# Splitting the last store of a pairwise product kernel into groups of 16 partitions

## Chip, cores, metric

One core of one Trainium2 chip. Times are device microseconds of a whole execution; lower is better. A verdict is "faster" or "slower" beyond 2%. The profile's span is some 1.8 us shorter than the timed execution of the same run.

## The reference

```python
# x: (4096, 32, 64) float32, W: (64, 64) float32
vid = jnp.einsum('bfd,de->bfe', x, W)
idx_i, idx_j = jnp.triu_indices(32, k=1)          # 496 pairs of fields
return x[:, idx_i, :] * vid[:, idx_j, :]          # (4096, 496, 64), 520 MB
```

Almost all the traffic is the result: 520 MB written, 34 MB read.

## The kernel before

A tile holds 256 rows of the batch: 128 partitions are 2 halves x 64 elements, and each pair of fields has 128 values (512 B) per partition. TensorE forms `vid` in PSUM, VectorE multiplies, and SP stores the products, 124 pairs at a time (63,488 B in each of 128 partitions) once the kernel is under way. Three output buffers are in rotation.

```python
    for t in range(NT):                       # 16 tiles of 496 pairs
        ...                                   # loads on the ACT queue, matmuls
        sent = 0
        for j in range(1, F):
            i = 0
            while i < j:
                ...                           # ot: [128, 124, 128], one of 3 buffers
                nc.vector.tensor_tensor(ot[...], xt[...], vid[...], ALU.mult)
                i += n
                at += n
                if t * NP + at == until or at in (base + SLOT, NP):
                    nc.sync.dma_start(
                        out=out[t][:, sent:at, :],
                        in_=ot[:, sent - base : at - base, :],
                    )
                    sent = at
```

## Time and profile before

| | before |
|---|---|
| time, median of the first 3 runs (least, most) | 1298.64 us (1297.97, 1299.37) |
| span of the profiled run | 1296.3 us |
| VectorE's waits for stores to free a buffer | 149.5 us in 52 waits |
| one row of 63,488 B on one DMA engine | 2.342 us, 27.1 B/ns |

The last row is from the trace's records of DMA packets. These, and the records of semaphore updates, give each transfer's shares of work (each of the 82 stores has 128 rows and 16 updates; a "share" is what stands behind one update, and is read as what one engine does of one transfer), though without the engines' numbers. The lines of the profile, and what they say of the end of the program, are in the prediction.

### The profile page before, as it was taken

What the parts mean: (1) busy time and instruction counts of PE and PEld (TensorE: products, weight loads), DVE (VectorE), ACT (ScalarE), POOL (GpSimd) and SP (SyncE); (2) the same over time, 40 slices, a digit from 0 to 9 for tenths busy, and PEclk for the clock granted to TensorE, in tenths of its full rate; (3) what the DMA queues carried; (4) which work ended last, traced back from release to release, by engine and by line L of the source; (5) the groups of instructions that cost most, each with busy time, mean ns of one, the idle gap of its engine ahead of it and who ended that gap; (6) DMA issues with size and microseconds to landing.
All of it is one profiled execution on the core that took longest, in us unless ns stands there. A gap on an engine that the chain in (4) does not pass through costs nothing.

```text
span 1296.3 us, 2062 instructions
## 1 busy us (share of the span) xinstructions
PE 225.5 (17%) x512; PEld 52.1 (4%) x512; DVE 1098.1 (85%) x544; POOL 0.2 (0%) x4
## 2 busy tenths in 40 slices
PE   4112131122121121211212112121121211212000
PEld 1000000000000000000000000000000000000000
DVE  7999999898798888988888888888888888979970
POOL 0000000000000000000000000000000000000000
PEclk8555555565555555655555565555555655555555
DMA  9999999999999999999999999999999999999996
GB/s 379 430 426 433 438 432 425 434 434 434 428 432 432 434 432 434 431 434 436 432 434 434 426 434 432 430 432 432 432 433 431 434 432 434 432 431 443 425 431 288
DMA packets 20891, 553.81 MB, mean 427 GB/s; under 512 B 2448, under 2 KB 2448, under 8 KB 10256
## 3 DMA queue, kind: packets, MB, share of 16 engines
q1 hardware_dynamic: 12816, 524.33, 93.8%
q10 hardware_dynamic: 8064, 29.36, 5.5%
q8 instruction: 4, 0.07, 0.0%
q14 instruction: 7, 0.06, 0.0%
HBM read 33.59 MB, written 520.09 MB: 427 GB/s over the span
## 4 chain that ended last, share of the span: by engine, by line
DMA 61%; DVE 34%; issue 1%; DVEq 0%; PE 0%; SPq 0%
DMA out_dram<-o 61%; DVE o L99 34%; DMA x<-in_r_x_dram 0%; DVEq L145 0%; PE pv L81 0%; DVEq L99 0%; SPq L56 0%
## 5 line engine op out<-in xcount | busy, mean ns | idle before, releaser
L99 DVE TENSOR_TENSOR o<-x,pv 128x2176 f32<-128x2176 f32 (+27 forms) x544 | 1098.1, 2093 | 158.3 <-DMA out_dram<-o 149.5
L81 PE MATMUL pv<-x,w 64*64 64x512 f32 x512 | 225.5, 1025 | 966.3 <-DMA x<-in_r_x_dram 887.2
L81 PEld LDWEIGHTS pv<-x,w 64*64 64x64 f32 x512 | 52.1, 208 | 1138.0 <-issue 1137.4
L128 POOL MEMSET const-bfloat16-1.0<- 128x1 bf16 x1 | 0.1, 102 | 0.0
L128 POOL MEMSET const-uint8-127<- 128x1 uint8 x1 | 0.1, 102 | 0.0
L128 POOL MEMSET const-float32-1.0<- 128x1 f32 x1 | 0.1, 99 | 0.0
L128 POOL MEMSET const-float32-0.0<- 128x1 f32 x1 | 0.1, 98 | 0.2 <-issue 0.2
## 6 DMA issues: line engine op xcount, KB each, us to landing
out_dram<-o SPq DMA_DIRECT2D x56, 7936.0 KB, 42.9
x<-in_r_x_dram ACTq DMA_DIRECT2D x56, 512.0 KB, 48.7
out_dram<-o SPq DMA_DIRECT2D x2, 3008.0 KB, 17.8
out_dram<-o SPq DMA_DIRECT2D x1, 5952.0 KB, 27.1
out_dram<-o SPq DMA_DIRECT2D x1, 4928.0 KB, 23.1
out_dram<-o SPq DMA_DIRECT2D x1, 4416.0 KB, 19.0
out_dram<-o SPq DMA_DIRECT2D x1, 4224.0 KB, 21.2
out_dram<-o SPq DMA_DIRECT2D x1, 3904.0 KB, 15.3
```

The lines of the kernel that those rows point to most:

```text
L81: nc.tensor.matmul(pv[half, :, :], lhsT=w2[half, :], rhs=xt[half, b : b + BANK, :], start=True, stop=True,)
L99: nc.vector.tensor_tensor(ot[:, at - base : at - base + n, :], xt[:, i : i + n, :], vid[j // BANK][:, j % BANK : j % BANK + 1, :].to_broad ...
L128: nc = _bacc.Bacc("TRN2", target_bir_lowering=False, num_devices=1, dynamic_dma_scratch_size=1024)
```

## The change

The change stores the last 124 pairs in eight groups of 16 partitions, each without its last 1 to 8 pairs, and deals those out in stores of 15 and 1, 14 and 2, ... 8 and 8 partitions. A small store leaves some engines out, and the change takes work from some and gives it to others, evidently so that they all end together. Where the texts say "high-numbered", take it as those that the small stores leave out.

```diff
+def steps(lo, hi):
+    for g in range(8):
+        yield lo, hi - g - 1, 16 * g, 16 * g + 16
+    for g in range(8):
+        yield hi - g - 1, hi, 16 * g, 16 * g + 15 - g
+        yield hi - g - 1, hi, 16 * g + 15 - g, 16 * g + 16
...
-                    nc.sync.dma_start(
-                        out=out[t][:, sent:at, :],
-                        in_=ot[:, sent - base : at - base, :],
-                    )
+                    last = t == NT - 1 and at == NP
+                    for lo, hi, p, q in steps(sent, at) if last else [(sent, at, 0, P)]:
+                        nc.sync.dma_start(
+                            out=out[t][p:q, lo:hi, :],
+                            in_=ot[p:q, lo - base : hi - base, :],
+                        )
```

## The prediction

> **What bounds the kernel now.** I read the page first, for the span, the strip of 40 slices and the bytes:
>
> ```profile
> span 1296.3 us, 2062 instructions
> PE 225.5 (17%) x512; PEld 52.1 (4%) x512; DVE 1098.1 (85%) x544; POOL 0.2 (0%) x4
> DMA  9999999999999999999999999999999999999996
> GB/s 379 430 426 433 438 432 425 434 434 434 428 432 432 434 432 434 431 434 436 432 434 434 426 434 432 430 432 432 432 433 431 434 432 434 432 431 443 425 431 288
> HBM read 33.59 MB, written 520.09 MB: 427 GB/s over the span
> ```
>
> The reader is to see that the DMA engines are 90% busy or more in every slice but the last, which falls to 6 tenths and 288 GB/s. VectorE, at 85%, waits for buffers that stores free. The kernel is bound by the DMA engines, and what the change touches is the end of the last slices. So next come the waits of the SP queue (who waited for whom: us in total, times, longest) and the timeline at the end:
>
> ```profile
> SPq L145 <- DMA out_dram<-o: 38.5, 1, 38.5
> ```
>
> ```profile
> 1239.46 16.95 DVE L99 TENSOR_TENSOR o<-x,pv 128x768 f32<-128x768 f32 x5 [1.69 <-DMA out_dram<-o]
> ```
>
> VectorE ends its last product at 1239.46 + 16.95 = 1256.41 us; after that SP does nothing but wait for the last store to land. How the 16 engines run out is in the busy table by windows (columns: window, length, PE, PEld, DVE, POOL, clock, DMA share, GB/s):
>
> ```profile
> 1260.00:1265.00 5.00, 0.00 (x0) 0.00 (x0) 0.00 (x0) 0.00 (x0) 0.50 1.00 432
> 1275.00:1280.00 5.00, 0.00 (x0) 0.00 (x0) 0.00 (x0) 0.00 (x0) 0.50 0.94 406
> ...
> 1284.00:1286.00 2.00, 0.00 (x0) 0.00 (x0) 0.00 (x0) 0.00 (x0) 0.50 0.37 159
> 1286.00:1288.00 2.00, 0.00 (x0) 0.00 (x0) 0.00 (x0) 0.00 (x0) 0.50 0.07 32
> 1288.00:1290.00 2.00, 0.00 (x0) 0.00 (x0) 0.00 (x0) 0.00 (x0) 0.50 0.22 95
> 1290.00:1291.00 1.00, 0.00 (x0) 0.00 (x0) 0.00 (x0) 0.00 (x0) 0.50 0.15 63
> ```
>
> (A window counts a packet where it starts, so shares jump.) From 1284 us on few engines still have work. The semaphore updates in the trace give it engine by engine: the 16 shares of the last store land from 1283.29 to 1295.48 us, eight of them by 1284.1, the last two at 1294.85 and 1295.48; their mean is about 1286.7. The store before it landed with the same pattern, from 1264.58 to 1276.76. So the engines are out of step by 12.2 us, the same in each of the last six stores, and the end is set by one slow engine that still has its eight rows to do. In the packet records each row of 63,488 B takes 2.342 us on one engine (27.1 B/ns), on slow engines too: they are late, not slower here. Perfect balance would be worth 1295.5 - 1286.7 = 8.8 us, 0.7%, and that is the ceiling of any gain at this end.
>
> The cost of an issue, from the view of the tensor that the stores write:
>
> ```profile
> L108 SPq DMA_DIRECT2D out_dram<-o x82: 332/332/348, 12.2 to 1256.4; - x82
> ```
>
> The three durations (least, median, most) are in ns: 332 for nearly all. The next SP instruction starts 0.38 us after an issue.
>
> [...] All 82 stores before have 128 partitions and land in 16 shares[...]. [...] The trace doesn't number its engines; it only shows that all 16 run at 27.1 B/ns together. [...]the first packet of the 32 KB weight load starts 1.0 us after its issue, and the last data packet's end to its landing is 0.35 us, so a small store should take some 1.45 us.
>
> **The change part by part.** One store of 128 rows x 124 pairs becomes 24: eight of 16 partitions with 123 down to 116 pairs, then for each group the last 1 to 8 pairs in two parts (15 and 1, 14 and 2, ... 8 and 8 partitions). Bytes, VectorE, TensorE and everything before 1256.4 us stay as they are; the compared orders of the two built programs show only SP gaining 22 rows.
>
> *Moved bytes.* With one partition to an engine, each engine gets eight leading rows of 956 pairs together instead of 992. [...] A pair is 512 B, 19 ns at 27.1 B/ns, so the most that a late engine is relieved of is 36 x 19 = 0.68 us. That is the gain, if the late engines are the high-numbered ones: the slowest would land its leading rows at about 1294.85.
>
> *New waits.* In the built program each store waits for the one that used its semaphore before, and there are eight: store 8 waits for the former last but one store (landed 1276.76), store 9 for store 1, and so on to store 24 for store 16. Before, such waits were few; they show as stores that wait for a load whose semaphore they reuse, though they need nothing of it:
>
> ```profile
> SPq L108 <- DVE o L99: 1168.4, 80, 22.2
> SPq L108 <- DMA x<-in_r_x_dram: 50.3, 5, 19.1
> ```
>
> Now store 8 is issued at about 1276.8 and its rows can start at 1277.8; the fast engines run out of the first seven at 1264.24 + 7 x 2.27 = 1280.1, so that is just hidden. But store 16 can go only when store 8 has landed on the slowest engine, 1294.9, and stores 17 to 24 follow at 0.385 us each: the last is issued at 1294.9 + 8 x 0.385 = 1298.0 and lands 1.45 us later, at 1299.5. Against 1295.5 that is +4.0 us: without anything else, 1298.6 + 4 = 1302.7 us.
>
> [...] Then the time is 1325 to 1338, about 1332 us.
>
> **Rivals.** (A) [...]my main theory, chance 0.68: 1325 to 1340. [...]against: no transfer of this trace has fewer than 128 partitions[...]. (B) An engine's rate is the only limit and the chain of semaphores sets the end, chance 0.27: 1302.7. For it: the waits are in the built program; the ports' effect is unseen here. (C) [...]1309 to 1318; chance 0.04. (D) The relief of the high engines is all that counts, and SP's issues are hidden: 1298; chance 0.01, since store 24 cannot be issued before store 16 has landed.
>
> **Range and chances.** 2% is 26 us, so slower begins at 1324.6. A gives slower nearly always, with a small part of it just below the line; B and C give the same; a gain over 2% would need three times the whole imbalance. I put the prediction at 1331 us, a little below the middle of A as B pulls the median down; the range 1300 to 1342 holds B's and A's values. Faster 0.01, same 0.33, slower 0.66.
>
> **What would show it.** For A: packets of some 62,000 B in the last 60 us that take 4 to 9 us in place of 2.34, a DMA share still high but GB/s near 110 to 200, the end of the span at about 1330. For B: packets at 2.3 us, the leading rows landing by 1295, SP waiting at the store line for earlier stores, a last issue at about 1298. In both, SP's waits for stores at the store line must appear. I am wrong if the last issue comes without waiting, if SP's issues of small stores cost far from 0.385 us, or if the slow engines' lag differs in the changed run.

The sum came to this: 1298.6 us for the kernel before; with 4.0 us for the chain of semaphores 1302.7 us; and, by the main theory, with 26 to 39 us (34 in the middle, the chain included) in place of the 4.0, 1325 to 1338, about 1332 us. The main theory (A), the ports theory, supposed that the engines slow one another when a store has few partitions.

## The result, and the profile after

The changed kernel takes 1320.47 us (median of 4 runs, 1317.48 to 1324.50) against 1298.76 us (4 runs), +21.7 us. The ratio is 1.017, with a 95% interval of 1.0141 to 1.0198: "same" by the 2% rule, but a clear loss. A ratio here is the mean time of one kernel's runs over that of the other's of the same rounds, so not quite the ratio of the medians.

The profiled run is the slowest of the four (1324.5 us). Its page shows where the time goes: the strip of 40 slices is as before until the last two, which move 269 and 109 GB/s where before they moved 431 and 288.

```profile
span 1322.7 us, 2085 instructions
DMA  9999999999999999999999999999999999999994
GB/s 379 427 426 433 439 436 427 427 448 427 427 429 450 424 427 428 449 427 426 425 445 430 425 432 444 426 428 432 440 425 427 437 439 425 429 445 430 432 269 109
```

The busy table by windows at the end, first of the kernel before, then of the changed kernel (columns as in the prediction, the last three are clock, DMA share and GB/s):

```profile
1264.00:1282.00 18.00, 0.00 (x0) 0.00 (x0) 0.00 (x0) 0.00 (x0) 0.50 1.03 444
```

```profile
1264.40:1282.00 17.60, 0.00 (x0) 0.00 (x0) 0.00 (x0) 0.00 (x0) 0.50 1.08 200
1282.00:1300.00 18.00, 0.00 (x0) 0.00 (x0) 0.00 (x0) 0.00 (x0) 0.50 0.89 237
1300.00:1318.00 18.00, 0.00 (x0) 0.00 (x0) 0.00 (x0) 0.00 (x0) 0.50 0.23 67
1318.00:1322.00 4.00, 0.00 (x0) 0.00 (x0) 0.00 (x0) 0.00 (x0) 0.50 0.28 55
```

This is the reading that matters most. From 1264.4 to 1282 us the engines are as busy as before (1.08 against 1.03), and they move less than half as much (200 against 444 GB/s). The first line starts 0.4 us earlier; from 1264.4 us on, the kernel before has 1.01 and 436 GB/s. A busy engine is not a fast one here: rows take longer. In the packet records, 84 of the 183 rows after 1258 us still run at 27 B/ns (37 of them before the first group's rows start); the others are slower and take up to 15.5 us in place of 2.3.

The waits of the SP queue show the second part of the loss:

```profile
SPq L119 <- DVE o L108: 1169.8, 80, 22.2
SPq L119 <- DMA x<-in_r_x_dram: 49.3, 5, 19.0
SPq L119 <- DMA out_dram<-o: 42.5, 8, 20.8
SPq L156 <- DMA out_dram<-o: 1.3, 4, 0.4
```

The third line is new: eight times SP waits at the store line (L119) for an earlier store, 42.5 us in all, where before it waited 38.5 us at the end of the program. These are the waits for a semaphore that is used again. The last of them ends when store 8 has landed on the last engine at 1317.45; store 16 is issued at 1317.47, store 24 at 1320.13, and it has landed at 1321.88.

### The profile page after: what moved, and what is told of

Its sections match the earlier page's. It is cut to its first block, busy times and chain, and to the rows that moved or that the text cites. A ratio compares the mean times of both kernels' runs of the same rounds, so it can differ in the third digit from the quotient of the medians.

```text
span 1322.7 us, 2085 instructions
## 1 busy us (share of the span) xinstructions
PE 225.8 (17%) x512; PEld 52.1 (4%) x512; DVE 1098.0 (83%) x544; POOL 0.2 (0%) x4
## 4 chain that ended last, share of the span: by engine, by line
DMA 60%; DVE 33%; issue 1%; DVEq 0%; PE 0%; SPq 0%
DMA out_dram<-o 60%; DVE o L108 33%; DMA x<-in_r_x_dram 0%; DVEq L156 0%; PE pv L90 0%; DVEq L108 0%; SPq L65 0%
```

## The experiments

Each replaces only `steps` (for e4 also the slice of partitions). All results were correct, and all timed runs of the fast state (e6 and e7 have one run each, of unknown state). Two questions: do the few partitions of each store make the loss (the ports theory), or the chain of semaphores; and why is the loss smaller than the estimate?

**e1: the groups alone, no split tails.**

```diff
-    for g in range(8):
-        yield lo, hi - g - 1, 16 * g, 16 * g + 16
-    ... (the tails)
+    for g in range(8):
+        yield lo, hi, 16 * g, 16 * g + 16
```

> The eight groups of 16 partitions with all 124 pairs each, and no split tails: eight stores in place of 24, so no store waits for one of the same last set. Ports theory [...]: most of the changed kernel's loss stays, 1298.7 + 16 to 23 = 1315 to 1322 us, with row packets of 4 to 9 us. Rival, the chain of semaphores makes the loss: 1298 to 1301 us, packets of 2.34 us.

Measured: 1317.81 us (1314.04 to 1321.24) against 1297.30, ratio 1.016 (1.0131 to 1.019). The engines are as slow as in the changed kernel:

```profile
1264.40:1282.00 17.60, 0.00 (x0) 0.00 (x0) 0.00 (x0) 0.00 (x0) 0.50 1.07 209
```

Nearly the whole loss is in the groups; the tails' few us can't be told from these two medians, as the runs of either kernel spread over 7 us.

**e2: the chain alone.** Again 24 stores, and each of the last 16 waits for the one eight before it, but the first eight are of 128 partitions, and every tail has 8 pairs.

```diff
+    n = hi - 8 - lo
     for g in range(8):
-        yield lo, hi - g - 1, 16 * g, 16 * g + 16
+        yield lo + g * n // 8, lo + (g + 1) * n // 8, 0, P
     for g in range(8):
-        yield hi - g - 1, hi, 16 * g, 16 * g + 15 - g
-        yield hi - g - 1, hi, 16 * g + 15 - g, 16 * g + 16
+        yield hi - 8, hi, 16 * g, 16 * g + 15 - g
+        yield hi - 8, hi, 16 * g + 15 - g, 16 * g + 16
```

> 24 stores with the same chain of waits, but the first eight are whole 128-partition stores of 14 or 15 pairs, and only the last 8 pairs go in groups split 15 and 1 to 8 and 8. Ports theory: the rows run at 27 B/ns, only the chain's end remains, stores 16 to 24 issued after the slowest engine's last row: 1298.7 + 3.5 to 5.5 = 1302 to 1304 us. Rival, the chain makes the loss: 1315 to 1322 us as in the changed kernel.

Measured: 1302.25 us against 1297.30 (runs 1302.37, 1303.08, 1294.94, 1302.13; the odd one is unexplained, it was not profiled), ratio 1.0024 (0.9992 to 1.0057), an interval that takes in no loss at all. Its SP waits and its window at the end:

```profile
SPq L120 <- DMA out_dram<-o: 38.4, 10, 18.3
```

```profile
1264.40:1282.00 17.60, 0.00 (x0) 0.00 (x0) 0.00 (x0) 0.00 (x0) 0.50 0.97 408
```

The waits are as long as in the changed kernel (38.4 against 42.5 us), but the engines run at 408 GB/s, and the loss is 5 us in three runs of four. A wait that lasts long costs only what lies after the engines' own work: here store 16 is issued at 1295.3, when the slowest engine's leading rows have landed, and store 24 lands at 1299.74, 4.5 us after them.

**e3: two stores of 64 partitions.**

```diff
+    yield lo, hi, 0, 64
+    yield lo, hi, 64, P
```

> The last store as two of 64 partitions. [...] Ports theory: a row of 63,488 B takes 3.3 to 4.7 us[...], the time is 1298.7 + 6 to 17 = 1305 to 1316 us. Rival, stores of few partitions or many small stores are slow in themselves: 64 partitions on 16 engines cost nothing, 1298 to 1300 us.

Measured: 1316.89 us (1314.49 to 1318.82), ratio 1.0153 (1.0137 to 1.017), 0.9 us above the expected range. In the packet records the commonest time of a slowed row is 4.95 us, 12.8 B/ns, a little under half of the 27.1 B/ns of the kernel before: 44 of the two stores' 128 rows take 4.85 to 5.05 us, and 36 run at full speed. No small store, no chain of waits, and still 19.6 us lost: nearly as much as the 20.5 us of e1, which has 16 partitions to a store.

**e4: groups of 16 partitions, every eighth one.**

```diff
+    for g in range(8):
+        yield lo, hi, slice(g, P, 8)
```

> Eight stores of 16 partitions as in e1, the same number, size and waits, but each takes every eighth partition[...]. Ports theory: [...]a loss clearly under that of e1: 1298.7 + 5 to 15 = 1304 to 1314 us. Rival, stores of 16 partitions are slow in themselves: the same as e1, 1315 to 1322 us.

Measured: 1313.70 us (1310.87 to 1314.62), ratio 1.0126 (1.011 to 1.0142), 4.1 us less than e1 with the same number and size of stores. The runs just overlap (1314.04 us is the least of e1, 1314.62 the most of e4), so the size of the difference is uncertain. What differs is only which 16 partitions a store takes, and with them which rows of the output it writes, so these places cost time.

**e5: which engines are late.** One store of 128 partitions, and the last 8 pairs in seven small ones.

```diff
+    yield lo, hi - 8, 0, P
+    p = 0
+    for n in (64, 15, 14, 12, 8, 8, 7):
+        yield hi - 8, hi, p, p + n
+        p += n
```

> One 128-partition store of 116 pairs, then the last 8 pairs in stores of 64, 15, 14, 12, 8, 8 and 7 partitions[...]. They queue behind each engine's own rows, so their landings say which engines are late. If the late ones are the high-numbered ones (which is what the change supposes): the shares that land last are missing from the stores on fewer engines, and the time falls by up to 1.2 us. If they are others: the last shares stay in the small stores. Time in both cases 1295 to 1300 us, as no store waits long.

Measured: 1300.51 us against 1298.52, ratio 1.0014 (0.9998 to 1.0031), 0.5 us above the range. The small stores land in 15, 14, 12, 8, 8 and 7 shares, one to a partition. Each small share lands 0.15 to 0.9 us behind the share before it on the same engine, so an engine that a store lacks shows as a missing late share. In this profiled run the last shares of the 64-partition store land at 1297.05, 1298.13 and 1299.31. The store of 15 partitions lacks the one after 1299.31: the engine that it leaves out is the latest. The store of 14 also lacks the one after 1297.05: the other engine that it leaves out is third. The share after 1298.13 is still there in the store of 7 partitions, where it lands at 1299.25: the second latest is among the seven engines of that store, where four more of the late ones are. These get more work from the change, if its small stores lie on the same engines as those of e5, which was not shown. So even where the engine that a store of 15 leaves out is the latest, relieving it gains at most 1.2 us. And it isn't so always: in e2's profiled run the two that land last are both in the store of 12 partitions.

**e6 and e7: the disputed cost by itself.** Eight stores of one pair come first; the eighth waits for the store before to land in full, so all engines begin the rest within 0.5 us of one another.

```diff
+    for g in range(8):
+        yield lo + g, lo + g + 1, 0, P
# e6
+    yield lo + 8, hi, 0, 64
+    yield lo + 8, hi, 64, P
# e7
+    for g in range(8):
+        yield lo + 8, hi, 16 * g, 16 * g + 16
```

> The disputed cost by itself, with engines that start together: eight stores of one pair, of which the eighth waits for the store before to land in full, then 116 pairs in two stores of 64 partitions. A row is 59,392 B, 2.19 us at 27.1 B/ns. Ports theory: [...]every row 4.5 to 4.7 us, 8 rows 36 to 38 us after about 1279, so the end near 1317 and a time near 1320 us. Rival, no sharing: rows 2.19 us and 1300 us.

> As the even start with halves, but the 116 pairs in eight stores of 16 neighbouring partitions[...]. Ports theory: [...]a row takes 8.7 to 9.3 us, 8 rows up to 74 us, the end at 1330 to 1353 and a time of 1333 to 1356 us[...]. Rival, no sharing: 1300 us.

Measured: 1317.35 and 1332.86 us (one run each, so of unknown state; the second 0.1 us under its range). The window of e6 that holds the first half's rows, then e7's first group and the seven others:

```profile
1277.50:1296.00 18.50, 0.00 (x0) 0.00 (x0) 0.00 (x0) 0.00 (x0) 0.50 1.00 205
```

```profile
1279.00:1288.10 9.10, 0.00 (x0) 0.00 (x0) 0.00 (x0) 0.00 (x0) 0.50 1.00 104
1288.10:1330.00 41.90, 0.00 (x0) 0.00 (x0) 0.00 (x0) 0.00 (x0) 0.50 0.75 159
```

All engines are 100% busy in the first window of each, at 205 and at 104 GB/s, where 128 partitions give 435. The packet records have the rows, each of 59,392 B:

| partitions of the store | one row | each engine | all engines |
|---|---|---|---|
| 128 (from 63,488 B in 2.342 us) | 2.19 us | 27.1 B/ns | 435 GB/s |
| 64 (e6) | 4.63 us | 12.8 B/ns | 205 GB/s |
| 16 (e7, first group) | 8.9 to 9.2 us | 6.5 B/ns | 104 GB/s |

When all engines work on one store of 64 partitions, each has 0.47 of its rate, and with 16 partitions 0.24: about the half and the quarter. What makes this was not shown. But e7 also shows what the estimate had wrong. In step, its eight rows would take 8 x 9.1 = 73 us; they took from 1279.0 to 1329.9, 51 us. The second group's rows, which all start within 0.33 us, already take from 6.2 to 8.7 us: they don't slow alike. The engines part, and one that is ahead can be at full speed again: the first row of the third group, alone in that group, takes 2.19 us. In the third group the shares land over 8 us (1296.9 to 1304.9).

**e8 and e9: the groups in another order, and e1 again beside it.**

```diff
-    for g in range(8):
+    for g in (0, 1, 4, 5, 2, 3, 6, 7):   # e8 (e9 is e1)
         yield lo, hi, 16 * g, 16 * g + 16
```

> The eight groups of 16 partitions as in e1, in the order 0, 1, 4, 5, 2, 3, 6, 7. [...] Ports theory with drift: [...]1 to 8 us less than the repeat of e1 in this call. If the loss comes from anything[...] (number of stores, their size, the issue): the same as the repeat, within 1.5 us.

> The kernel of e1 again, on the same chip as the changed order, for comparison: 1298 + 16 to 22 = 1314 to 1320 us.

Measured: e8 1312.20 us (1308.26 to 1317.83), ratio 1.0115 (1.0077 to 1.0153); e9 1319.71 us (1317.44 to 1323.59), ratio 1.0164 (1.0142 to 1.0185). The same stores in another order lose 7.5 us less by the medians; one of e8's four runs lies within e9's range, and the two intervals overlap, so the size of this is uncertain. Why one order should cost less was not shown. The profiled runs agree that it does, e8's first and then e9's:

```profile
1264.40:1282.00 17.60, 0.00 (x0) 0.00 (x0) 0.00 (x0) 0.00 (x0) 0.50 1.12 296
```

```profile
1264.40:1282.00 17.60, 0.00 (x0) 0.00 (x0) 0.00 (x0) 0.00 (x0) 0.50 1.09 213
```

Of the rows that start after 1264.4 us, 68 of 148 keep full speed in e8 and 48 of 147 in e9, and the slowest takes 9.3 us in place of 16.6.

No experiment points to a version that beats the kernel before: all keep its bytes, and the best of them, e5, is 0.1% behind.

## Why the prediction was right or wrong

**The range held (1300 to 1342), the loss is where the theory put first has it, in stores of few partitions, and its size was too large:** 1331 was said and 1320.5 came, 32 us of loss against 21.7. That the range held owes something to luck: it reached from rival B's time to the main theory's, and 1320.5 lies between, in no theory's own stretch (C's ends at 1318, the main theory's begins at 1325). The likeliest class, slower by over 2% (0.66), did not come: "same" (0.33) did, as the loss of 1.7% lies just under the line.

- *Ports.* Right in kind: in e6 and e7 rows run at 12.8 and 6.5 B/ns, nearly the half and the quarter of 27.1, and e3 loses 19.6 us with no small store at all. That ports are the cause was not shown. The step that failed is that a group's engines slow one another equally, and with it the term of 26 to 39 us. Less the chain's 4.6 us, which was part of it, the groups were to cost 21 to 34 us. In the profiled run, the slowest, the leading rows have landed at 1317.45 where 1294.85 was worked out without such slowing: 22.6 us. The other runs end 3.4 to 7 us earlier, so the groups cost some 16 to 19 us there (an estimate that takes their chain to be as long). What the runs showed in place of that is e7: engines that part after one row, 51 us in place of 73.
- *The chain of semaphores.* Right in its waits and its end. From store 8's landing on the last engine to store 24's landing 4.65 us were worked out; it was 4.43 in the changed kernel, and some 4.5 in e2. A small store was to land 1.45 us after its issue; one of a pair, with nearly all engines idle, took 1.5 us in e7. The tail's stores start every 0.33 us, not 0.385. As the whole cause (rival B), it is refuted by e1, where it is absent, and by e2, where it is all there is.
- *Store 8's wait.* Mis-sized: it was to end at 1276.8 and ended at 1289.19, since the latest engine's last six rows of the former store took 3.3 to 5.1 us each in place of 2.34, while other engines were already in the groups: the store before landed over 24.4 us, and the ones before it over 12.4. That cost little: the first engine has its seventh row landed at 1289.32, and the first share of store 8 lands at 1292.62.
- *SP's issues.* Stores 2 to 7 took SP 1.2 to 4.1 us each, not the 0.332 that the stores before took; the view of the store line gives 4107 ns as the longest. They are hidden behind the queued rows: the last of them ends at 1268.4, when the first row of store 1 is just landing (1268.5).
- *Relief of late engines.* The 0.68 us ceiling was not tested by itself; e5 shows that what it aims at holds only in part, with five of the late engines among those in its smallest store.
- *Rival C* (the same loss, but milder) is refuted by the table: a row took 4.63 us in e6 and 8.9 to 9.2 us in e7, as the main theory expected (4.5 to 4.7 and 8.7 to 9.3). Its time, 1309 to 1318, was near the truth for another reason.
- *Small slips of the working.* The mean landing of the last store is 1286.4 us, not 1286.7, so perfect balance would be worth 9.1 us and not 8.8; SP gains 23 stores (82 to 105), not 22 rows. None of them changes the outcome.

**A rival not separated.** In every experiment a store's partitions of SBUF and its rows of the output in HBM change together. So the runs show that fewer partitions to a store slow the engines, to about the half and the quarter (12.8 and 6.5 B/ns of 27.1), but not that the limit is on the SBUF side: the place of the written rows was not varied alone.

Open: why the rows of one group slow so unequally (6.2 to 8.7 us in e7's second), why engines fall behind one another through the kernel at all, and why the changed kernel's runs differ by 7 us where those of before differ by 1.4.

## What to carry to other kernels

In this case a store's partitions decide how fast it runs, not only its bytes and its engines: with all engines on stores of 128, 64 and 16 partitions they moved 435, 205 and 104 GB/s, while the profile showed them fully busy each time. So look at GB/s beside the busy share. If a store has to be split, split it along the free dimension, with all 128 partitions in each part: e2's eight such parts kept 408 GB/s, where e1's groups of 16 had 209. Before steering work to some engines, find out which are late and by how much (here 12.2 us from the first to the last). And count the semaphores: with the eight of this program in rotation, a store waits for the one eight before it, which came to 42.5 us at the store line.
